# Softmax sums added up by DMA, and edge bits transposed off the matrix engine: one change to a four-layer graph kernel

## The chip, the core and the metric

The kernel runs on one core of a Trainium2 chip. A core has five engines that run their own instruction streams: TensorE (PE, matmuls; its weight loads are listed as PEld), VectorE (DVE), ScalarE (ACT), GpSimd (POOL) and SyncE (SP, which here only issues DMAs). PE writes into eight PSUM banks; the others work in SBUF and PSUM. The metric is the device time of one execution in microseconds: 2737.14 us, the median of three runs (2736.57 to 2737.26).

## The reference

64 graphs of 256 nodes with 256 features pass through four layers, each followed by `x = layernorm(x + layer(x, adj))`. Layer 0 is a transformer block with 8 heads of 32; the changed lines lie in its attention:

```python
allowed = (adj > 0) | (jnp.swapaxes(adj, 1, 2) > 0) | eye
qkv = x @ Wqkv.T + bqkv
scores = jnp.einsum('bhqd,bhkd->bhqk', q * scale, k)
scores = jnp.where(allowed[:, None], scores, -jnp.inf)
attn = jax.nn.softmax(scores, axis=-1)
ctx = jnp.einsum('bhqk,bhkd->bhqd', attn, v)
x = _layernorm(x + ctx @ Wo.T + bo, ln1_g, ln1_b)
ff = jax.nn.relu(x @ W1.T + b1) @ W2.T + b2
x = _layernorm(x + ff, ln2_g, ln2_b)
```

Layers 1 and 2 are single-head graph attention (a softmax over `leaky_relu(f_i + g_j)` where there is an edge), layer 3 is two relational graph convolutions. All products are f32. The mask `allowed` needs the edge matrix and its transpose.

## The kernel before

One graph is two row tiles of 128 nodes. `graph(g)` (line 757) writes down the operations of one graph: load, masks, attention, `wo`, layer norm, feed forward, two graph attention layers (`gat`), two convolutions (`conv`), the last layer norm and the store. Each operation goes into a `Plan` (line 128) with its engine, an assumed cost, the tiles it reads and writes and, for DMAs, a size and a lag. When all 64 graphs are written down, `Plan.schedule` orders them: it takes on each engine the operation with the smallest due time (`DUE`, one number for each kind of operation, plus `LATER`, one for each graph), no more than `WINDOW` ahead of the oldest, as soon as its buffers in the rings (`RINGS`, `SMALL`, `DRAM`) are free. PE's modes (`full`, `row`, `col`, `bits`, ...) carry assumed costs of switching. The instructions then stand in that order in each engine's queue, and every queue is executed in order. Seven to eight graphs are in flight at once, so that at any time PE works on matmuls of several layers of different graphs.

What the change touches:

- `masks` (901): `bits = adj > 0` in bf16 (DVE, L906); PE transposes its four 128x128 blocks into a bank `pt` (L911); `gm` (L914, for the graph attention layers) and `am = max(pt, bits)` (L915), then the diagonal (L920).
- `attention` (953): the scores are computed transposed (keys on partitions), eight heads in two groups `kt` of key tiles (L969, four row tiles of 32x128 side by side). ACT takes the exponential (L975), DVE multiplies by the mask (L977). `both[r]` is the sum over the two key tiles (L982, four DVE adds). `values` (987) is one PE operation: for each half `hg` of the heads four matmuls by a matrix of ones, 128 rows by 32 columns, which add `both` over the 128 partitions and put the sum on 32 partitions for each head (L991), then eight matmuls with `v` (L996). DVE takes the reciprocal of all 128x256 sums of each half (L1002) and multiplies (L1003). An ACT pass over `inv` (L1005) collects a number that is checked at the end of the program.
- `feed_forward` (1017): `x1` is turned for the next product, then multiplied by `ln1g` (L1022 by way of `with_row`, L782) and `b2` is added by DVE (L782 again).
- Helpers that the text speaks of: `add_later` and `add_row_later` (785, 789) add by a DMA with `accum_op=add`, issued by POOL (L787). `bounced` (818) transposes a tile without PE: DVE turns 32x32 blocks (L824), a DMA writes them to DRAM (`rows`, L827) and another reads them back in the right order (`T`, L832). `product` (870) issues all dense matmuls, so they all stand under L873. `layer_norm` (875) has four small POOL instructions (L887 to L890).

Of the kernel before, what the change touches and what calls it, by code (L numbers as in the profile page):

```python
# [11 lines left out]
BF16 = mybir.dt.bfloat16  # L12
# [14 lines left out]
FIRST_TURNED = 2  # L27
# [6 lines left out]
RINGS = {"x": 3, "adj": 4, "bits": 2, "am": 2, "gm": 6, "T": 4, "qk": 2, "v": 2, "p": 12, "both": 4, "inv": 1, "ctxT": 2, "X": 8,  # L34
         "xr": 1, "hid": 1, "h": 3, "e": 3, "n": 1, "rel": 3, "hi": 2, "lo": 2, "o": 4, "blocks": 1, "turned": 1, "xT": 2, "cols": 2, "pf": 3}
DRAM = {"rows": 8, "row": 6}
SMALL = {"mv": 8, "st": 4, "rstd": 8, "r": 6, "rdeg": 4}


WORTH, HOLD, WAIT, LOCK = 20.0, 0.0, 1000000.0, -0.5  # L40
WINDOW, FIRST, TAIL = 4.0, 6, 58
LANES = 8
DUE = [
    115.11, 130.1, 87.27, 113.55, 184.78, 267.91, 127.15, 3.7, 6.4, 850.28, 907.96, 17.01, 767.99, 288.87, 535.33, 276.68, 323.52, 314.8, 295.86, 329.82,
    300.15, 372.49, 286.87, 287.98, -502.68, 591.19, 64, 190.54, 194.31, 213.9, 713.3, 602.04, 241.89, 284.25, 282.43, 286.42, 332.5, 286.53, 340.1, 391.1,
    -896.08, 82.57, 223.73, 1512.3, 652.66, -43.08, 40.01, 326.22, 390.1, 385.75, 460.35, 501.93, 1085.72, 819.32, 729.09, 1434.36, 1462.97, 1572.86, 309.27, 377.7,
    422.98, 298.61, 489.54, 349.1, 349.77, 403.91, 409.77, 1039.63, 1164.93, 1206.11, 1047.88, 1793.82, 1345.99, 941.63, 462.04, -143.68, -426.28, -563.2, -305.02, 262.4,
    -8.54, -682.53, -1425.23, -878.48, -910.48, 17.76, -1230.15, -1241.9, -450.83, -995.94, -1138.75, -609.23, -940.48, -121.13, -36.53, 517.96, -269.05, 397.54, 54.48, 413,
    377.06, 153.19, 158.68, -378.26, 790.96, -31.03, 404.99, 300.98, 1238.57, 734.43, 1000.75, 626.51, 101.96, 382.13, 45.13, 270.56, -211.2, 112.91, -26.02, 715.95,
    909.95, 879.4, 1800.2, 738.61, -248.98, -17.6, 171.18, 86.17, 653.43, -436.69, 887.7, -60.25, 1415.03, -622.37, 760.39, 726.88, -39.87, 361.21, 51.78, -354.13,  # L50
    -811.15, -996.74, -21.07, -458.08, -355, -638.8, -301.25, -345.83, 35.99, -729.94, 342.61, 978.89, 501.93, 624.52, -156.62, 34.99, -355.8, -535.26, -1056.55, -853.61,
    -309.82, -604.29, -123.96, -430.91, 250.59, -935.54, -71.5, 785.28, 299.06, 741.23, 514.78, 1612.86, 44.41, -201.89, -507.28, 48.76, -1134.8, -1513.38, -738.99, -2121.1,
    -1887.25, -2427.69, -1547.71, -1074.55, -1743.55, -801.23, -1039.08, -1445.41, -1451.37, -1811.92, -1599.65, -1352.15, -803.41, 105.4, 51.2, -2.45, 905.11, 340.42, 479.09, 446.27,
    -346.11, -241.48, -1320.8, -1184.67, 227.95, -410.93, 181.58, 411.97, 33.28, 533.62, 973.02, 416.68, 625.02, -116.64, 219.42, -238.55, -103.18, 369.86, -1126.9, -254.14,
    -62.97, -478.61, -760.52, 195.37, 133.89, -1164.69, -221.19, 309.39, -223.51, -1384.43, -912.86, -586.25, -502.37, -752.61, -194.22, -177.7, -903.8, -82.98, 212.44, 450.15,
    -20.63, 600.03, 718.67, -372.99, -463.15, -655.56, -114.2, -441.38, -98.81, -1186.92, 2.55, 33.89, -212.9, 343.42, -941.93, -141.06, 434.71, -230.33, -762.23, -500.28,
    -737.15, -1236.95, 350.32, -429.54, 392.55, 735.93, -165.46, 17.17, -406.76, -280.33, -545.61, -118.67, -562.59, -662.05, -637.17, -123.17, -299.09, -894.99, -728.14, 308.8,
    -407.46, -591.06, -1279.97, -1171.47, -1185.92, -532.14, -839.14, -1199.67, -1382.19, -1710.49, -1500.13, -823.47, -1317.15, -1651.44, -1534.52, -1542.11, -1999.83, -2099.36, -2677.74, -1674.04,
    -2031.11, -886.93, -741.03, 141.07, -201.09, -665.49, -899.61, -1034.61, -519.13, 753.8, -330.91, 224.95, -439.11, -74.6, -388.8, 150.07, 320.46, 266.34, 661.45, -131.11,
    -575.29, -614.71, -909.95, -860.38, -218.26, -502.7, 299.21, -466.82, -157.72, -96.09, 95.71, -751.12, -80.72, -711.21, -1440.05, -1626.75, -1496.54, -701.82, -2131.37, -1553.57,  # L60
    -767.95, -883.9, -451.78, -721.17, -77.66, -81.75, -876.87, -264.16, -284.81, 164.33, 500.84, 572.97, 751.67, 221.66, -573.04, -421.79, -309.92, 661.24, -78.37, 822.6,
    402.49, 814.87, 925.8, 120.82, 1121.82, 521.23, 871.11, 987.71, 661.55, 675.71, 250.34, -481.05, -752.44, -688.49, -790.45, -353.78, -477.33, -799.05, -598.48, -834.15,
    135.16, 359.04, -419.04, -153.16, -427.9, -63.74, 206.11, 144.64, -396.59, 87.54, -508.49, 33.99, 247.18, -231.56, 116.24, 559.54, 113.68, 945.19, 114.83, 632.95,
    846.63, 23.88, 241.92, -60.66, 167.66, 426.06, -250.81, -25.85, -886.96, 163.03, 213.44, 144.25, -197.06, 214.87, 469.41, 48.09, 314.49, 729.23, 840.48, 272.15,
    949.87, -274.06, 407.94, 518.88, 627.68, -253.81, -324.22, 788.98, 182.1, 73.25, -283.59, -278.9, -438.37, -351.07, -11.1, 234.91, 791.22, 267.52, -262.82, 221.58,
    -55.85, -273.21, -716.88, -232.74, -243.65, -337.37, -686.64, 243.63, -363.44, 102.34, -294.19, 157.49, -122.58, 818.8, 167.06, -139.62, 564.19, 183.5, 40.04, 561.24,
    -469.96, -301.06, 183.9, -432.22, 344.47, -19.44, 175.22, -329.23, 111.52, 31.67, 0, 12.49, 16.35, 40.7, 13.03, 29.97, 79.66, 87.72, 88.16, 92.57,
    16.9, 42.2, 63.91, 67.37, 69.2, 69.57, 64.77, 66.51, 67.73, 68.1, 54.65, 63.05, 66.15, 90.74, 93.34, 103.29, 93.94, 113.24, 100.44, 111.1,
    101.32, 106.37, 89.66, 91.55, 102.68, 90.95, 92.88, 92.14, 95.53, 92.74, 96.15, 112.62, 115.22, 115.84, 108.16, 120.58, 126.02, 128.08, 123.52, 127.74,
    128.55, 132.38, 133.45, 134.52, 135.25, 136.34, 139.84, 156.74, 162.92, 141.05, 141.83, 146.74, 158.73, 159.93, 153.03, 155.22, 160.92, 162.78, 158.68, 159.54,  # L70
    161.3, 162.04, 154.36, 156.09, 161.67, 162.41, 156.95, 157.81, 160.55, 163.15, 165.1, 168.73, 172.37, 173.1, 174.18, 178.53, 179.69, 180.41, 181.13, 184.82,
    188.33, 190.19, 190.97, 195.88, 202.19, 203.65, 203.07, 206.36, 222.82, 225.76, 209.06, 211.91, 217.09, 223.82, 225.27, 228.89, 231.63, 234.38, 242.79, 245.03,
    235.73, 243.83, 244.01, 246.19, 248.14, 251.65, 257.58, 258.36, 263.28, 272.62, 274.23, 269.16, 273.95, 276.54, 341.81, 276.37, 276.67, 281.05, 288.88, 287.58,
    292.81, 294.47, 301.47, 303.32, 303.53, 307.8, 309.41, 309.85, 304.06, 309.25, 311.17, 313.08, 313.83, 318.66, 320.01, 324.08, 327.59, 217.6, 300.09, 321.45,
    331.08, 331.85, 336.77, 350.16, 352.09, 353.9, 355.27, 348.44, 350.37, 351.98, 353.57, 356.31, 359.28, 360.19, 360.79, 357.08, 357.99, 359.21, 361.32, 361.85,
    365.25, 366.27, 367.05, 374.16, 388.51, 395.12, 397.74, 400.66, 385.92, 388.51, 398.17, 401.4, 402.41, 406.64, 404.62, 407.66, 408.19, 415.16, 418.79, 420.65,
    446.91, 460.58, 469.56, 476.66, -42.08, -71.22, 47.55, 3.95, 87.01, -47.02, 84.87, 96.85, 43.29, 49.34, 127.81, 93.06, 163.1, 82.32, 60.43, 233.39,
    93.62, 90.44, -0.5, 120.06, -23.99, 59.25, 35.15, -243.24, 80.37, 53.47, 200.92, -73.58, -7.08, 5.9, -5.15, 25.23, 43.87, 9.22, -39.39, -39.72,
    -111.42, -25.63, 15.17, 9.26, 110.12, -23.73, 207.1, 32.19, 46.32, 175.57, 73.87, -13.49, 97.45, -54.1, 63.07, 26.32, 36.13, -21.71, 254.66, 142.72,
    97.69, 92.02, 135.98, 306.53, 204.66, 18, 8.92, 47.55, 119.05, -168.79, 195.29, 2.68, 311.48, 151.91, 107.66, 214.4, 509.65, 39.08, 110.14, 228.99,  # L80
    218.6, 168.24, 162.95, 261, 207.45, 107.57, 85.27, 116.9, 164.82, 190.13, 200.94, 178.43, 163.52, 204.35, 300.87, 365.21, 103.17, 173.45, 85.86, 207.98,
# [267 lines left out]
def tile_gnn_stack(ctx: ExitStack, tc: tile.TileContext, t: dict, out: bass.AP):  # L349
# [267 lines left out]
    def main_path(plan):  # L617
# [139 lines left out]
        def graph(g):  # L757
# [117 lines left out]
            def layer_norm(y):  # L875
# [21 lines left out]
                dve(0.88, stats, [y], [mv, stat])  # L897
                op("POOL", 1.8, root, [mv], [rstd], port="waits", lag=0.15)
                act(1.0, apply, [y, rstd], [y])

            def masks(adj):


# [570 lines left out]
```

## Time and profile before

| | |
|---|---|
| median of three runs | 2737.14 us |
| the profiled execution | 2740.2 us, of which its span 2738.3 us |
| PE / DVE / ACT / POOL busy | 99% / 90% / 58% / 34% of the span |
| sums by ones, L991 | 1024 records, 379 to 404 ns each |
| transposes of bits, L911 | 256 records, 219 ns |
| reciprocal, L1002 | 128 x 1729 ns |
| row adds and products, L782 | 192 x 671 to 672 ns |
| adding DMAs on POOL, L787 | 190, mean issue 942 to 1618 ns, landing 3.8 to 4.6 us after issue |
| DMA packets | 609611, mean 120 GB/s |

How to read it: the profile is one execution. Records of PE overlap, because matmuls are pipelined, so the distance from one start to the next says more than a record's length. An f32 matmul leaves two records, a bf16 one a single one. A list of waits gives, for an engine's instruction and the one that released it, the total in us, how many times, and the longest. A line of the timeline has start, duration, engine, line, operation, what it writes and reads, shape and count.

### The profile page before, as it was taken

Reading aid. Unit: us, or ns where it says so; the run is one execution under the profiler, and the core shown is the slowest. Engines: PE = TensorE matmul, PEld = TensorE weight load, DVE = VectorE, ACT = ScalarE, POOL = GpSimd, SP = SyncE. Lnnn points to the kernel's source line nnn. Section 1 sums busy time; section 2 is a strip of 40 time slices with the busy share of each in tenths; the row PEclk is TensorE's granted clock in tenths of the full one; section 3 lists DMA queues with packets and bytes.
Section 4 is the critical chain, followed back from the end, with each engine's and each line's share of the span. In section 5 each row is a group of like instructions: output and inputs, shape, how many; then the busy total and the mean of one; then the engine's idle time right before and its main releaser. Section 6 shows DMA issues by size and latency. Waiting matters only on the chain.

```text
span 2738.3 us, 48644 instructions
## 1 busy us (share of the span) xinstructions
PE 2712.7 (99%) x15808; PEld 2115.7 (77%) x15808; DVE 2465.2 (90%) x6538; ACT 1598.4 (58%) x3830; POOL 935.5 (34%) x1747
## 2 busy tenths in 40 slices
PE   8999999999999999999999999999999999999997
PEld 6887877777787787777777877877877777778774
DVE  6789989999999999999999999999999999988977
ACT  4446555556556556556555565565565555655767
POOL 2233333334333333333333333343333333332222
PEclk8999999999999999999999999999999999999999
DMA  7345545454454454554544544544545546364211
GB/s 187 95 110 130 130 116 129 119 127 123 127 135 120 128 130 121 129 124 129 133 120 124 139 119 125 135 121 127 129 121 132 125 128 147 97 143 108 51 47 40
DMA packets 609611, 329.91 MB, mean 120 GB/s; under 512 B 391694, under 2 KB 600616, under 8 KB 609352
## 3 DMA queue, kind: packets, MB, share of 16 engines
q1 hardware_dynamic: 564984, 275.72, 36.1%
q0 software_dynamic: 44368, 51.01, 11.9%
q8 instruction: 128, 2.10, 0.3%
q14 instruction: 131, 1.07, 0.1%
HBM read 182.60 MB, written 94.23 MB: 101 GB/s over the span
## 4 chain that ended last, share of the span: by engine, by line
PE 97%; DVE 1%; DMA 1%; ACT 1%; issue 0%; SPq 0%; POOL 0%; POOLq 0%
PE bank L873 80%; PE bank L969 5%; PE bank L1155 4%; PE bank L996 4%; PE bank L991 2%; PE bank L911 1%; DMA wqkv<-in_WqkvT_dram 0%; PE bank L802 0%; DMA rows<-turned 0%; ACT turned L813 0%; DVE p L977 0%; ACT e L1170 0%; DMA T<-rows 0%; DVE inv L1002 0%; ACT X L894 0%
## 5 line engine op out<-in xcount | busy, mean ns | idle before, releaser
L887 POOL TENSOR_SCALAR rstd<-mv 128x2 f32<-128x2 f32 x384 | 148.7, 387 | 1415.1 <-DVE mv L884 469.0
L873 PE MATMUL bank<-cw,T 128*128 128x512 f32 x1024 | 469.0, 592 | 0.0
L873 PE MATMUL bank<-T,w 128*128 128x256 f32 x2048 | 466.6, 380 | 0.0
L873 PE MATMUL bank<-w,hid 128*128 128x256 f32 x2048 | 457.0, 381 | 0.0
L873 PEld LDWEIGHTS bank<-w,hid 128*128 128x128 f32 x2048 | 397.0, 196 | 43.0 <-issue 3.4
L873 PEld LDWEIGHTS bank<-T,w 128*128 128x128 f32 x2048 | 384.8, 190 | 53.8 <-issue 2.0
L975 ACT ACTIVATE p<-bank 128x512 f32<-128x512 f32 x512 | 298.8, 603 | 169.9 <-PE bank L969 169.7
L894 ACT ACTIVATE X<-X,rstd 128x256 f32<-128x256 f32 x640 | 350.0, 599 | 78.1 <-POOL rstd L890 77.3
L977 DVE TENSOR_TENSOR p<-p,am 128x512 f32<-128x512 f32 x512 | 336.6, 681 | 27.4 <-ACT p L975 22.8
L888 POOL TENSOR_TENSOR rstd<-rstd,neghalf 128x2 f32<-128x2 f32 x384 | 315.0, 820 | 32.0
L873 PEld LDWEIGHTS bank<-cw,T 128*128 128x128 f32 x1024 | 198.8, 195 | 164.5 <-issue 144.8
L1031 ACT ACTIVATE hid<-bank,col_b 128x256 f32<-128x256 f32 x512 | 212.5, 469 | 105.3 <-PE bank L873 104.1
L873 PE MATMUL bank<-h,e 128*128 128x259 f32 x1024 | 264.3, 382 | 0.0
L873 PE MATMUL bank<-gw,T 128*128 128x258 f32 x1024 | 255.1, 381 | 0.0
L873 PE MATMUL bank<-xT,wqkv 128*128 128x256 f32 x1024 | 253.7, 385 | 0.9 <-DVE xT L865 0.9
L1002 DVE RECIPROCAL inv<-bank 128x256 f32<-128x256 f32 x128 | 217.2, 1729 | 30.7 <-PE bank L996 30.5
L882 DVE BATCH_NORM_STATS2 st<-X 128x6 f32<-128x256 f32 x640 | 238.3, 414 | 2.2
L873 PEld LDWEIGHTS bank<-gw,T 128*128 128x128 f32 x1024 | 198.8, 196 | 46.3 <-issue 24.6
L873 PEld LDWEIGHTS bank<-h,e 128*128 128x128 f32 x1024 | 186.5, 190 | 46.4 <-issue 14.9
L873 PEld LDWEIGHTS bank<-xT,wqkv 128*128 128x128 f32 x1024 | 193.0, 192 | 30.6 <-issue 2.5
L1155 PE MATMUL bank<-hi,rel 128*128 128x258 f32 (+1 forms) x512 | 182.6, 364 | 0.1
L824 DVE STREAM_TRANSPOSE turned<-X 128x512 f32<-128x512 f32 x236 | 166.1, 704 | 4.6 <-ACT X L894 3.1
(147 smaller groups left out, 4676.9 us busy)
## 6 DMA issues: line engine op xcount, KB each, us to landing
rows<-turned SPq DMA_DIRECT2D x295, 256.0 KB
T<-rows SPq DMA_DIRECT2D x295, 256.0 KB
adj<-in_adj_dram SPq DMA_DIRECT2D x128, 256.0 KB
x<-in_x_dram SPq DMA_DIRECT2D x64, 256.0 KB
xr<-in_x_dram SPq DMA_DIRECT2D x64, 256.0 KB
x<-row_bo POOLq DMA_DIRECT2D x64, 256.0 KB, 4.5
xr<-row_ln_b POOLq DMA_DIRECT2D x64, 256.0 KB, 3.8
out_dram<-o SPq DMA_DIRECT2D x64, 256.0 KB
```

The lines of the kernel that those rows point to most:

```text
L824: dve(0.63, lambda: nc.vector.transpose(turned().rearrange("p k (b n i) -> p (k b) i n", b=4, i=NB), xt().rearrange("p i (j c) -> p j i c" ...
L873: nc.tensor.matmul(dst, lhsT=lhs(c), rhs=rhs(c), start=(c == 0), stop=(c == n - 1))
L882: nc.vector.bn_stats(stat()[:, i, :], y()[:, i, :])
L887: nc.gpsimd.tensor_scalar(rstd()[:, 0, :], mv()[:, :, 1], 1.0, EPS, op0=ALU.mult, op1=ALU.add)
L888: nc.gpsimd.tensor_tensor(rstd()[:, 0, :], rstd()[:, 0, :], neghalf[:, 0:NB], op=ALU.pow)
L894: nc.scalar.activation(y()[:, i, :], y()[:, i, :], AF.Identity, bias=rstd()[:, 1, i : i + 1], scale=rstd()[:, 0, i : i + 1])
L969: nc.tensor.matmul(s[r]()[:, hg, :], lhsT=qk()[f, KB + hg, kt * P : (kt + 1) * P], rhs=qk()[f, hg, :], start=True, stop=True)
L975: act(0.58, lambda pr=pr, k=k, sr=s[r]: nc.scalar.activation(pr(), sr(), AF.Exp, accum_out=seen_sum[:, k : k + 1]), [s[r]], [pr])
L977: dve(0.60, lambda pr=pr, kt=kt: nc.vector.tensor_tensor(pr(), pr(), am()[:, kt, None, :].to_broadcast([P, KB, N]), op=ALU.mult), [pr, am] ...
L1002: dve(1.67, lambda hg=hg, pc=pc: nc.vector.reciprocal(inv()[:, hg, :], pc()[:, 1, :]), [pc], [(inv, hg)])
L1031: act(0.36, lambda f=f, k=k, ph=ph: nc.scalar.activation(hid()[:, f + k, :], ph()[:, k, :], AF.Relu, bias=b1[:, f + k : f + k + 1]), [ph, ...
L1155: nc.tensor.matmul(pa()[:, 0:n], lhsT=rel()[:, i, j * P : (j + 1) * P], rhs=part()[:, i, 0:n], start=(c == 0), stop=(c == len(terms) - 1))
```

## The change

1. **Sums.** `both` is now one tile that holds the four adds side by side. Two adding DMAs on POOL ("folds") add, for the first half of the heads, partitions 64 to 127 onto 0 to 63, and for the second half the other way. The sums matmuls then have 64 rows instead of 128 (the first half on rows 0 to 63, the second on 64 to 127), and all eight stand ahead of the values.
2. **Reciprocal.** The sums are the same on 32 partitions, so DVE transposes them in 32x32 blocks (two instructions), takes the reciprocal of one column of each block (128x16) and spreads the result with one more block transpose. ACT's pass reads the 128x16 tile.
3. **Bits.** From graph 4 on, PE no longer transposes `bits`. `bits_bounced` turns 32x32 blocks on DVE (two instructions), writes them to DRAM (`rows_b`) and reads them back (`pt`, in runs of 32 bf16 numbers, 64 bytes). `gm` and `am` then read `pt` from SBUF.
4. **b2** is added by a DMA (`add_row_later`) in place of a DVE add.
5. **Rings and order.** `both` 4 to 1 (of four times the size), `p` 12 to 11, `adj` 4 to 3, `pf` 3 to 2, `inv` gives way to `sums` (2) and `compact` (3), `turned_b` and `pt` 1 each, `rows_b` 4. `WORTH`, `HOLD`, `WINDOW`, all of `DUE` and `LATER` have new numbers, so the order of instructions on every engine is a new one.

```diff
-FIRST_TURNED = 2
+FIRST_TURNED, FIRST_BOUNCED = 2, 4
...
-WORTH, HOLD, WAIT, LOCK = 20.0, 0.0, 1000000.0, -0.5
-WINDOW, FIRST, TAIL = 4.0, 6, 58
+WORTH, HOLD, WAIT, LOCK = 38.41, 0.28, 1000000.0, -0.5
+WINDOW, FIRST, TAIL = 20.8, 6, 58
...
+            def bits_bounced(bits):
+                turned, rows, pt = new("turned_b", [P, NB, NB, P], BF16), new("rows_b", [4, P, P], BF16), tok("pt", BF16)
+                for k in range(NB):
+                    dve(0.35, lambda k=k: nc.vector.transpose(
+                        turned()[:, k].rearrange("p h (j c) -> p j h c", j=4),
+                        bits()[:, :, k * P : (k + 1) * P].rearrange("p h (a j) -> p j h a", j=4)), [bits], [(turned, k)], "uses")
+                op("SP", 0.5, lambda: nc.sync.dma_start(rows().rearrange("m p x -> p m x"),
+                                                        turned().rearrange("p k h x -> p (k h) x")), [turned], [rows],
+                   lag=SENT, size=0.5)
+                def back():
+                    r = rows()
+                    nc.sync.dma_start(pt().rearrange("p k (m c) -> p (k m) c", c=32),
+                                      bass.AP(tensor=r.tensor, offset=r.offset, ap=[[32, P], [32 * P, 16], [1, 32]]))
+                op("SP", 0.5, back, [rows], [pt], lag=BACK, size=1.1)
+                return pt
...
+                if g < FIRST_BOUNCED:
...
+                else:
+                    pt = bits_bounced(bits)
...
-                both = [new("both", [P, KB, N]) for r in range(4)]
+                both, half = new("both", [P, KB, 4, N]), P // 2
...
+                for hg in range(KB):
+                    into, out_of = slice(half * hg, half * hg + half), slice(half - half * hg, P - half * hg)
+                    op("POOL", 1.3, lambda hg=hg, into=into, out_of=out_of: nc.gpsimd.dma_start(
+                        both()[into, hg], both()[out_of, hg], accum_op=ALU.add),
+                       [(both, r) for r in range(4)], [(both, "lo" if hg else "hi")], lag=2.4, size=0.9)
...
                 def values():
                     for hg in range(KB):
+                        rows = slice(half * hg, half * hg + half)
+                        for r in range(4):
+                            nc.tensor.matmul(pcs[hg]()[32 * r : 32 * r + 32, 1, :], lhsT=ones[rows, :], rhs=both()[rows, hg, r, :],
+                                             start=True, stop=True)
+                    for hg in range(KB):
                         pc = pcs[hg]()
-                        for r in range(4):
-                            nc.tensor.matmul(pc[32 * r : 32 * r + 32, 1, :], lhsT=ones, rhs=both[r]()[:, hg, :],
-                                             start=True, stop=True)
...
-                pe("col", 2.58, values, [v] + both + list(p.values()), pcs, [ctxT, inv])
+                pe("col", 2.15, values, [v, both] + list(p.values()), pcs, [ctxT, compact])
                 for hg in range(KB):
                     pc = pcs[hg]
-                    dve(1.67, lambda hg=hg, pc=pc: nc.vector.reciprocal(inv()[:, hg, :], pc()[:, 1, :]), [pc], [(inv, hg)])
+                    dve(0.40, lambda hg=hg, pc=pc: nc.vector.transpose(sums()[:, hg, :], pc()[:, 1, :]), [pc], [(sums, hg)])
+                dve(0.17, lambda: nc.vector.reciprocal(compact(), sums().rearrange("p k (j d) -> p (k j) d", d=32)[:, :, 0]),
+                    [sums], [compact])
+                dve(0.63, lambda: nc.vector.transpose(inv().rearrange("p k n -> p (k n)"),
+                                                      compact()[:, :, None].to_broadcast([P, KB * N // 32, 32])),
+                    [compact], [inv], "uses")
...
-                act(0.62, lambda: nc.scalar.activation(inv(), inv(), AF.Identity, accum_out=seen_inv[:, g : g + 1]), [inv], [inv])
+                act(0.3, lambda: nc.scalar.activation(compact(), compact(), AF.Identity, accum_out=seen_inv[:, g : g + 1]),
+                    [compact], [compact])
...
-                with_row(x1, b2, ALU.add, [c_b2])
+                add_row_later(x1, b2, [c_b2])
```

## The prediction

> **What bounds the kernel now.** I read the shares of the engines first, then a table by stretches, then the list of what TensorE (PE) waited for, and last the timeline of one attention step.
>
> ```profile
> PE 2712.7 (99%) x15808; PEld 2115.7 (77%) x15808; DVE 2465.2 (90%) x6538; ACT 1598.4 (58%) x3830; POOL 935.5 (34%) x1747
> ```
>
> ```profile
> 400.00:2200.00 1800.00, 1800.00 (x10541) 1409.14 (x10540) 1660.14 (x4392) 1052.92 (x2550) 652.39 (x1166) 1.00 0.51 127
> ```
>
> ```profile
> PE bank L873 <- DMA wqkv<-in_WqkvT_dram: 3.8, 2, 2.3
> PE bank L873 <- DVE xT L865: 3.4, 2, 2.5
> PE bank L911 <- DVE bits L906: 2.0, 1, 2.0
> PE bank L802 <- ACT turned L813: 1.6, 4, 0.8
> ```
>
> The second fence gives stretch, length and the busy time of PE, PEld, DVE, ACT and POOL, then PE's clock, DMA share and GB/s. From 400 to 2200 us PE is busy for all 1800 us, at a granted clock of 1.00; asked for the same stretch, the list of PE's waits is empty. "Busy" alone proves little for pipelined matmuls, but the starts do: from one dense 128x256 record to the next is 0.216 us, without gaps, and the scores of successive graphs start 41.74 us apart. So in the middle a graph costs what PE's records take to issue, and the waits that the third fence begins (13.8 us in all, at the start and end) are the rest. What leaves PE's stream comes off the time, as long as nothing new makes PE wait. DVE is next: 1660.14/1800 x 41.74 = 38.5 us per graph.
>
> ```profile
> 1017.38 0.64 PE L991 MATMUL bank<-both,ones 128*32 128x256 f32 x8
> 1017.83 1.05 PE L996 MATMUL bank<-p,v 128*32 128x256 f32 x16
> 1018.70 0.61 PE L991 MATMUL bank<-both,ones 128*32 128x256 f32 x8
> 1019.13 1.05 PE L996 MATMUL bank<-p,v 128*32 128x256 f32 x16
> 1020.11 0.40 PE L911 MATMUL bank<-ident_b,bits 128*128 128x128 bf16 x4
> 1020.34 0.87 PE L873 MATMUL bank<-w,hid 128*128 128x256 f32 x3
> ```
>
> An f32 matmul is two records. The x8 of L991 are four matmuls side by side in four column tiles: the next line starts 0.45 us later (1017.38 to 1017.83), and 0.43 us later in the second group (1018.70 to 1019.13). So a group of four costs one slot of 0.432 us, and a graph has six slots here: two of sums, four of values.
>
> **The sums (64 graphs).** Two sums slots become one: eight matmuls of 64 rows x 32 columns, the two halves on different rows and different banks. That removes 0.432 us. The row tiling of the scores shows four tiles of 32 rows side by side (L969, starts 7 ns apart), the sums show four of 32 columns; no row has both at once. What is new is a change of tile shape inside the step, from 64x32 to 128x32. It has no row. Its lower end is 0. Its upper end is entering the row tiling: the start-to-start step grows from 0.216 to 0.309 us, and the next from 0.196 to 0.300: 0.197 us. The nearest row is entering the column tiling, where the same two steps are 0.309 and 0.220: 0.093 + 0.024 = 0.117 us, which I take. A gain beyond 0 has no reason. So 0.432 - 0.117 = 0.315 us a graph, 64 x 0.315 = 20.2 us (bounds 0.235 and 0.432: 15.0 and 27.6). [...]
>
> **The bits (60 graphs).** Four bf16 transposes leave PE. From the last column-tiled start to the second dense start is now 0.311 + 0.067 + 3 x 0.056 + 0.277 = 0.823 us. In eleven places where dense work follows the values directly it is 0.309 + 0.329 = 0.638. So 0.185 us a graph, 60 x 0.185 = 11.1 us; the four starts alone (0.235) would give 14.
>
> **What is added beside PE, per graph.** DVE loses two reciprocals of 1.729 (L1002) and one row add of 0.671 (L782, b2): -4.13. It gains four 128x256 transposes, priced between the 128x64 row (0.226) and the 128x512 row (0.704): 0.43 each, 1.72; a broadcast transpose, 0.704; a reciprocal of 16 columns, between 0.153 (1 column) and 1.729 (256): 0.25. Sum +2.67, net -1.46: 37.0 us against a period of 41.2, so DVE stays hidden. If each 128x256 transpose took the full 0.704 it would be 38.1, still hidden. gm and am read SBUF in place of a bank, at 0.414 and 0.390 at most as now. ACT loses 0.4 us.
>
> POOL gains three adding DMAs (two folds, b2), each 0.94 to 1.62 us by the L787 rows: about 3.9, from 15.1 to 19 us. SP gains two DMAs of 0.36 us each; in the new order they stand among the row and T bounces, and a T read queued behind them waits for 'rows_b' to land. DMA: by mean packet times of the trace, 512 packets of 256 B at 17.9 ns, 2048 of 64 B at about 11 (4 B take 9.0, 128 B 12.1), 256 adding ones of 1 KB at 106.5 and 128 of 4 KB at 2 x 203: 9 + 22 + 27 + 52 = 110 us over 16 engines, 6.9 us. The share goes from 51% to about 68%. [...]
>
> **The new wait.** The values on PE now wait for the second fold, not for the last DVE add. In the middle of the trace the first sums matmul starts 5.3 us after the last 'both' add ends. The built program's instruction order shows DVE with 35 instructions between that add and the first transpose of the sums: six statistics (0.414), six aggregates (0.173), four 512-wide ones near 0.67, two 512-wide transposes near 0.70, ten 256-wide ones near 0.45, three more near 0.41 and four small ones near 0.15: 14.0 us by their rows. Less 2.6 us for sums and values themselves, the fold has about 11.3 us. It needs a first issue of 1.3 us and a landing of 4.9 (o<-X, median; longest 6.3): 6.2 us, longest 7.6. So some 4 to 5 us of cover. Behind the folds on POOL stand a layer norm's four instructions and the b2 add; behind the waiting sums on PE stands everything. The bits have nearly a graph's time to come back: gm stands some 100 DVE instructions after the second transpose of its bits.
>
> From x1's product to the first w1 matmul the new order holds 17.0 us of PE work, priced by the rows, against 19.1; from a graph's first matmul to its last, some 327 both times. That 2.1 us is the thinnest cover that shrinks.
>
> **Sum.** 20.2 + 11.1 = 31.3 us. The profiled execution took 2740.2 us (span 2738.3), so it would take 2708.9. The median of the runs shown is 3.1 us lower (2737.1), and gives 2705.8. I leave the start and the end of the program at 0: there chains of ACT and DVE set the pace, with 2 us either way.
>
> **Rivals.** (1) The 64-row halves do not run side by side. For: no row shows eight tiles at once. Against: rows and columns each run four tiles at once. Then the eight take 0.864 and the change of shape stays: +7.5 us, less 11.1: 2733.5. This is the case that the change does not do what it says. (2) The fuller DMA rings make the bounced T tiles late, as in the 2.1 us above, and PE waits a little. For: 51% to 68%, and PE's queue is in order. Against: now SP waits 317 us in all for 'rows' to land (L832), and PE not once for a T read that came of it. A wait of 0.3 us in 60 graphs: +18, 2723.8. (3) Slower: the folds are late. Ahead of them on POOL stands the adding DMA to xr, which waits for its load; the list of waits has it at 27.3 us in 6 waits, longest 9.0. If the folds land more than 11.3 us after the last add, PE stands still for the excess in each graph: it decides from 5.1 us of delay, eats the whole gain at 5.6, and at 6.1 (1 us of excess in 58 graphs) gives 2764. Against: six such waits in 64 graphs.
>
> **Chances.** Forecast, PE still packed, 2698 to 2714: 0.60. Late bounces, about 2724: 0.14. No overlap of the halves, about 2734: 0.12. Late folds, over 2743: 0.14. About 0.2% (5.5 us) is what a measurement here can tell from no change: under 2731.6 faster 0.74, up to 2742.6 same 0.12, slower 0.14. The range goes from 2696 (shape change free, 2705.8 - 7.4, and 2 us at the end) to 2736 (takes in the second and third case), and leaves out 0.14.
>
> **What the next profile shows.** Right: PE busy 1800 of 1800 in the middle, the graphs 41.2 us apart, sums of a graph in x16 records within 0.45 us, the first value record 0.3 us after the second pass of the sums. Wrong about the halves: two groups of sums 0.43 us apart. Wrong about covers: waits of PE with T<-rows (bounces) or both<-both (folds) as releasers, in every graph. DVE above 39 us per graph, or POOL above 24, would show a mispriced term.

## The result and the profile after

The changed kernel takes 2750.94 us (median of 6 runs, 2745.96 to 2752.70) where the kernel before takes 2737.18 (6 runs, 2736.57 to 2737.46): ratio 1.0047, 95% interval 1.0036 to 1.0058. It is slower by 13.8 us; the forecast was 2706. The profiled execution took 2751.08 us, span 2749.3.

First the shares of the engines, then the stretches asked for in the prediction with the start and the end of the program beside the middle (columns as there):

```profile
PE 2697.2 (98%) x15568; PEld 2078.2 (76%) x15568; DVE 2369.8 (86%) x6722; ACT 1552.7 (56%) x3830; POOL 1062.6 (39%) x1939
```

```profile
0.00:100.00 100.00, 76.71 (x520) 57.98 (x521) 54.10 (x137) 34.69 (x98) 26.41 (x43) 0.86 0.75 167
400.00:2200.00 1800.00, 1793.98 (x10430) 1393.16 (x10432) 1604.84 (x4542) 1020.41 (x2555) 717.57 (x1305) 1.00 0.69 153
2400.00:2749.30 349.30, 330.33 (x1755) 242.49 (x1746) 277.17 (x833) 220.62 (x481) 118.90 (x243) 0.98 0.39 87
```

The kernel before, asked for its first 100 us:

```profile
0.00:100.00 100.00, 88.86 (x610) 69.73 (x614) 67.84 (x145) 46.53 (x131) 24.69 (x41) 0.91 0.59 151
```

PE's total fell by only 15.5 us, and its idle time doubled, from 25.6 to 52.1 us of the span. In the first 100 us PE is busy for 76.7 us instead of 88.9, with a lower clock (0.86 against 0.91), and the DMA engines are busier (0.75 against 0.59). The middle is nearly packed, with 6 us missing. So the loss lies mostly outside the stretch that the prediction was worked out from.

The list of PE's waits over the whole program begins:

```profile
PE bank L1031 <- DMA both<-both: 11.8, 7, 4.8
PE bank L944 <- DVE bits L937: 8.4, 1, 8.4
PE bank L682 <- DMA T<-in_b_dram: 4.3, 1, 4.3
PE bank L1031 <- DVE X L1160: 2.1, 1, 2.1
PE bank L884 <- DMA T<-rows: 1.8, 5, 0.8
```

The waits for the folds (L1031) are few, seven in 64 graphs. Three of them, 7.3 us, lie before 100 us. The step itself does what was forecast. In the middle of the trace of after:

```profile
987.29 0.66 PE L1031 MATMUL bank<-both,ones 64*32 64x256 f32 x16
987.88 1.93 PE L1038 MATMUL bank<-p,v 128*32 128x256 f32 x32
```

All 16 records of the sums start within 0.28 us (eight starts 6 to 7 ns apart, 0.194 us, eight more), so eight 64x32 tiles run side by side. The values follow 0.59 us after the first start.

The table places the time. The ratios are against executions of the kernel before made beside each run, whose medians lie between 2736.99 and 2737.98. "g14" is the start of graph 14's sums in the timeline, "14-56" the time from there to graph 56's, "tail" the rest of the span. "Step" is the usual distance from one graph's sums to the next one's. The parts come from one profiled execution each. Executions of the changed kernel differ by 6.7 us among themselves, so a part is good to a few us only.

| kernel | median us (runs) | ratio to before, 95% | g14 | 14-56 | tail | step |
|---|---|---|---|---|---|---|
| before | 2737.18 (6) | | 558.3 | 1751.0 | 428.9 | 41.73 |
| after | 2750.94 (6) | 1.0036 to 1.0058 | 571.6 | 1742.9 | 434.9 | 41.28 |
| rows_moved | 2746.25 (7) | 1.0023 to 1.0046 | 573.1 | 1738.0 | 432.1 | 41.28 |
| no_fold | 2740.87 (10) | 1.0005 to 1.0024 | 557.7 | 1750.2 | 429.3 | 41.55 |
| no_bounce | 2736.69 (10) | 0.9986 to 1.0005 | 568.9 | 1735.2 | 431.6 | 41.28 |
| rows_nofold8 | 2735.92 (10) | 0.9986 to 1.0005 | 561.0 | 1739.2 | 438.0 | 41.28 |
| nofold14 | 2731.38 (10) | 0.9970 to 0.9989 | 559.8 | 1737.3 | 431.8 | 41.29 |
| flat_back | 2741.90 (10) | 1.0011 to 1.0030 | 569.6 | 1735.3 | 431.9 | 41.29 |
| pt_on_act | 2744.90 (9) | 1.0016 to 1.0037 | 573.2 | 1736.7 | 433.4 | 41.29 |
| bare_order | 2739.50 (10) | 0.9997 to 1.0016 | 561.8 | 1746.1 | 429.1 | 41.55 |
| nofold14_pt | 2731.34 (11) | 0.9970 to 0.9988 | 558.7 | 1735.9 | 429.5 | 41.29 |
| ends_pt | 2729.28 (7) | 0.9960 to 0.9982 | 562.1 | 1737.7 | 429.4 | 41.29 |
| ends_pt_sp | 2732.58 (11) | 0.9974 to 0.9992 | 563.3 | 1736.9 | 429.8 | 41.29 |
| before_rows_early | 2740.68 (11) | 1.0004 to 1.0022 | 558.4 | 1751.0 | 429.0 | 41.73 |
| fold_unwaited | 2748.13 (5) | 1.0029 to 1.0057 | 566.9 | 1748.6 | 430.9 | 41.55 |
| ends_pt_rows | 2729.62 (6) | 0.9957 to 0.9981 | 560.8 | 1737.7 | 429.2 | 41.29 |
| ends6_pt_rows | 2732.43 (11) | 0.9967 to 0.9985 | 561.9 | 1737.9 | 431.9 | 41.29 |

Had the step's gain of 0.45 us a graph come off everywhere, after would show 552, 1732 and 425. So this execution lost about 20 us before graph 14, 11 between 14 and 56, and 10 in the tail.

### The profile page after: what moved, and what is told of

The parts are those of the page before. It is cut to its first block, busy times and chain, and to the rows that moved or that the text cites. A ratio compares the mean times of both kernels' runs of the same rounds, so it can differ in the third digit from the quotient of the medians.

```text
span 2749.3 us, 48921 instructions
## 1 busy us (share of the span) xinstructions
PE 2697.2 (98%) x15568; PEld 2078.2 (76%) x15568; DVE 2369.8 (86%) x6722; ACT 1552.7 (56%) x3830; POOL 1062.6 (39%) x1939
## 4 chain that ended last, share of the span: by engine, by line
PE 86%; DVE 5%; DMA 4%; issue 2%; ACT 1%; POOL 1%; SPq 0%; POOLq 0%; DVEq 0%; ACTq 0%
PE bank L884 72%; PE bank L1038 4%; PE bank L1004 4%; PE bank L1205 4%; DMA both<-both 2%; PE bank L1031 1%; DMA T<-rows 1%; DVE p L1012 1%; DVE both L1017 1%; DMA rows<-turned 1%; DVE st L893 0%; DMA o<-X 0%; PE bank L813 0%; DVE turned L835 0%; DVE X L1064 0%
## 5 line engine op out<-in xcount | busy, mean ns | idle before, releaser
L898 POOL TENSOR_SCALAR rstd<-mv 128x2 f32<-128x2 f32 x384 | 112.1, 292 | 976.7 <-DVE mv L895 874.5
L1012 DVE TENSOR_TENSOR p<-p,am 128x512 f32<-128x512 f32 x512 | 331.0, 680 | 14.4 <-ACT p L1010 11.9
L899 POOL TENSOR_TENSOR rstd<-rstd,neghalf 128x2 f32<-128x2 f32 x384 | 302.2, 787 | 32.0
L1021 POOL DMA_DIRECT2D both<-both x128 | 110.0, 999 | 384.6 <-DVE rdeg L1211 148.8
L1081 ACT ACTIVATE hid<-bank,col_b 128x256 f32<-128x256 f32 x512 | 218.1, 472 | 68.9 <-PE bank L884 68.1
L884 PE MATMUL bank<-h,e 128*128 128x259 f32 x1024 | 255.6, 383 | 0.3 <-ACT e L1136 0.3
L884 PEld LDWEIGHTS bank<-h,e 128*128 128x128 f32 x1024 | 192.2, 190 | 44.8 <-issue 10.5
L1192 ACT CAST hi<-bank 128x256 fp32r<-128x256 f32 x256 | 94.8, 372 | 172.8 <-PE bank L884 172.3
```

Of the source, the lines that this page charges most:

```text
L884: nc.tensor.matmul(dst, lhsT=lhs(c), rhs=rhs(c), start=(c == 0), stop=(c == n - 1))
L898: nc.gpsimd.tensor_scalar(rstd()[:, 0, :], mv()[:, :, 1], 1.0, EPS, op0=ALU.mult, op1=ALU.add)
L899: nc.gpsimd.tensor_tensor(rstd()[:, 0, :], rstd()[:, 0, :], neghalf[:, 0:NB], op=ALU.pow)
L1012: dve(0.60, lambda pr=pr, kt=kt: nc.vector.tensor_tensor(pr(), pr(), am()[:, kt, None, :].to_broadcast([P, KB, N]), op=ALU.mult), [pr, am] ...
L1021: op("POOL", 1.3, lambda hg=hg, into=into, out_of=out_of: nc.gpsimd.dma_start(both()[into, hg], both()[out_of, hg], accum_op=ALU.add), [(b ...
L1081: act(0.36, lambda f=f, k=k, ph=ph: nc.scalar.activation(hid()[:, f + k, :], ph()[:, k, :], AF.Relu, bias=b1[:, f + k : f + k + 1]), [ph, ...
```

## The experiments

All of them except before_rows_early are edits of the changed kernel that keep its plan and the order of each engine's queue, apart from what is named. The first theory was that the early row loads lose the start, since the trace showed the first adjacency late behind them. The rivals were the folds and the bounces.

### rows_moved: the row loads put back

```diff
-        for o in plan.schedule():
-            o.issue()
+        for o in rest[:place] + late[:3] + rest[place:sums] + late[3:] + rest[sums:]:
+            o.issue()          # late: loads of ln1_b, b2, cb2 (at 24 us), sum of b2 (at 45 us)
```

> The changed kernel with one thing put back: the three row loads (ln1_b, b2, cb2) that its order issues on POOL at 5.6 to 6.7 us are issued at about 25 us, as before, and the small DVE sum of b2 after them; nothing else is moved. Theory 1, the lost time is lost at the start: the early row loads hold the DMA engines from 6 to 16 us, the first adjacency lands 14 us late (bits at 18.2 us instead of 4.2), PE's first dense work comes at 19.1 us instead of 8.8. Then the waits bank<-DVE bits (8.4 us) and bank<-T<-in_b (4.3 us) go, the dense work starts near 9 us, and the time falls by some 8 to 12 us, to about 2741. Theory 2, the loss is the folds' and the bounces': the start catches up later, because the first graphs wait for their own chains anyway, and the time stays at 2749 to 2752.

2746.25 us, 4.7 under the changed kernel, with overlapping intervals. The wait for bits fell from 8.4 to 1.6 us, but a wait for wqkv of 3.8 us came in its place, and graph 14 was no earlier (573.1). The first theory fell as the main cause: another load was now the late one. The 8.4 us are in part that one execution's: in no_fold and nofold14, whose instructions are the same up to there, the wait for bits is 3.1 us.

### no_fold: the folds out

```diff
-    nc.gpsimd.dma_start(both()[into, hg], both()[out_of, hg], accum_op=ALU.add)
+    None
-    lhsT=ones[rows, :], rhs=both()[rows, hg, r, :]
+    lhsT=ones, rhs=both()[:, hg, r, :]
```

> The changed kernel, same order on every engine, but the two folds issue nothing and the sums take all 128 rows again, as two groups. Nothing else differs. PE gets its slot back: the values step rises from 2.35 to 2.62 us, 64 x 0.267 = 17.1 us. If PE is packed and the folds are covered: 2751 + 17 = 2768, less the 11.8 us that PE waits for folds in four places: 2756. If the folds and their transfers are what makes the kernel slow (contention, late T reads), the time falls under 2751 in spite of the longer step, to 2745 or less.

2740.87 us: 10 us faster, although every graph takes 0.27 us longer (step 41.55). Graph 14 comes 13.9 us earlier. The folds cost more than they bring: 10.1 + 64 x 0.27 = 27 us, against the 17 us of the shorter step.

### no_bounce: the bounces of the bits out

```diff
-    pt = bits_bounced(bits)            # two DVE transposes, write, read-back
+    # same operations in the plan, nothing issued; gm and am read a constant of ones in place of pt
```

> The changed kernel, same order, but from graph 4 on the two block transposes of the bits and their two transfers issue nothing; both masks read a constant of ones instead, so the masks of these graphs are left out. DVE loses 0.9 us and the DMA engines some 31 us of packets per graph. Theory 1 (the start is the cause): the time stays within 2 us, 2749 to 2751, less the 1.8 us of waits for rows. Theory 2 (the bounces crowd the transfers, 64 B pieces above all): the middle's waits go, and the time falls by 6 us or more, to 2745 or less.

2736.69 us: 14 us faster. Graph 14 stays late (568.9); the gain is in 14-56, which has 1.4 us above a step of 41.28 in place of 9.1, and the tail. So folds and bounces seem to do their harm in different places. How much of the 9.1 is the bounces' own is not shown: rows_moved and nofold14 have the same instructions between graphs 14 and 56 as the changed kernel, bounces and folds included, and stand 4.2 and 3.5 us above the same sum.

### rows_nofold8: the row loads back, and folds only from graph 8 on

```diff
+    # as rows_moved, and:
-    both()[into, hg], both()[out_of, hg], accum_op=ALU.add)
+    both()[into, hg], both()[out_of, hg], accum_op=ALU.add) if g >= 8 else None
-    lhsT=ones[rows, :], rhs=both()[rows, hg, r, :]
+    lhsT=ones[rows, :] if g >= 8 else ones, rhs=both()[rows if g >= 8 else slice(0, P), hg, r, :]
```

> The three row loads put back to 25 us, and in graphs 0 to 7 the folds issue nothing and the sums take 128 rows; graphs 8 to 63 fold. The first folds wait some 8.5 us on PE in the changed kernel, because with few graphs in flight nothing covers a fold's 6 us. Eight graphs pay 0.267 us each, 2.1 us. Theory 1: 6 us under the run with the row loads alone, about 2735. Rival: these waits hide others (the chains of the first graphs, DVE and ACT), so only the 2 us are paid and the time is that of the other run or 2 us more.

2735.92 us, 10.3 under rows_moved: theory 1. Graph 14 comes at 561.0 instead of 573.1.

The timeline shows what the first two folds do to PE. After, around graphs 0 and 1:

```profile
43.37 2.29 PE L759 MATMUL bank<-spread_ln_b,w 128*128 128x1 f32 x20
47.22 1.20 PE L1031 MATMUL bank<-both,ones 64*32 64x256 f32 x16 [1.56 <-DMA both<-both]
48.36 3.64 PE L1038 MATMUL bank<-p,v 128*32 128x256 f32 x32
...
67.80 1.08 PE L1031 MATMUL bank<-both,ones 64*32 64x256 f32 x8 [4.79 <-DMA both<-both]
69.86 1.08 PE L1031 MATMUL bank<-both,ones 64*32 64x256 f32 x8 [0.99 <-DMA both<-both]
70.87 3.10 PE L1038 MATMUL bank<-p,v 128*32 128x256 f32 x32
```

The same step of graph 0 without folds (no_fold):

```profile
44.06 1.07 PE L1030 MATMUL bank<-both,ones 128*32 128x256 f32 x16
44.95 1.91 PE L1037 MATMUL bank<-p,v 128*32 128x256 f32 x32
```

The brackets hold the idle time and its releaser. A wait of 1.6 to 6 us is not all: the 32 values records behind it take 3.64 and 3.10 us instead of 1.91. The stretches around the first wait (columns: PE busy, clock, DMA share, GB/s) say why:

```profile
44.00:46.00 2.00, 1.66 (x15) 1.00 1.22 219
46.00:53.00 7.00, 5.78 (x60) 0.51 1.05 285
53.00:56.00 3.00, 3.00 (x32) 1.00 0.64 160
```

The clock granted to PE was halved (0.50) from 46.0 to 52.8 us. It fell during the wait, and not after it: PE stood still for only 1.56 us, behind 2.3 us of one-column matmuls (L759). The wait by itself does not decide it. In two other runs the same place looks as follows, first in bare_order (no folds, so no wait), then in flat_back (folds as in the changed kernel):

```profile
44.05 1.94 PE L1022 MATMUL bank<-both,ones 128*32 128x256 f32 x16
45.75 2.74 PE L1029 MATMUL bank<-p,v 128*32 128x256 f32 x32
```

```profile
45.71 0.76 PE L1031 MATMUL bank<-both,ones 64*32 64x256 f32 x16 [1.32 <-DMA both<-both]
46.40 1.93 PE L1038 MATMUL bank<-p,v 128*32 128x256 f32 x32
```

Without a wait the sums of bare_order took 1.94 us and the values 2.74, where no_fold's took 1.07 and 1.91; from the first start of the sums to that of the values it is 1.70 us instead of 0.89, about half the pace. With a wait of 1.32 us the sums of flat_back took 0.76 us and the values 1.93, close to the 0.66 and 1.93 of the changed kernel's middle. So the wait neither suffices nor is needed; what else decides it is not shown. At the second fold of the changed kernel, with 4.8 and 1.0 us of waiting, the clock was 0.50 from 67.8 to 73.0 us.

The folds themselves, on DVE and POOL of after:

```profile
34.30 2.49 DVE L1017 TENSOR_TENSOR both<-p 128x512 f32<-128x512 f32 x4
37.10 0.92 POOL L1021 DMA_DIRECT2D both<-both  x1 [29.87 <-DVE both L1017]
37.67 2.85 POOL L798 DMA_DIRECT2D x<-row_bo  x2
39.16 2.28 POOL L1021 DMA_DIRECT2D both<-both  x1
```

The adds end at 36.8 us and the sums can start at 47.2: 10.4 us for a fold that the prediction put at 6.2, with the second issue taking 2.28 us. Between the two issues stand two other adding DMAs of POOL (`x<-row_bo`), and from 40 to 48 us the DMA share (packet times added up, over the time of 16 engines) is 1.15: the first graphs' and weights' loads are under way. How much of the 10.4 us each of these makes up is not shown. In the middle the same rows are:

```profile
1019.26 0.67 DVE L1017 TENSOR_TENSOR both<-p 128x512 f32<-128x512 f32 x1
1020.49 1.69 POOL L1021 DMA_DIRECT2D both<-both  x2 [6.60 <-DVE rdeg L1211]
1029.30 0.66 PE L1031 MATMUL bank<-both,ones 64*32 64x256 f32 x16
```

From the end of the adds PE's sums follow after 9.4 us here (9.2 in the median of graphs 14 to 55), and the second fold has landed after 7.0 in the median: some 2 us to spare, where the prediction counted on 4 to 5.

### nofold14: folds only from graph 14 on, row loads left early

```diff
+    # as the fold lines of rows_nofold8, with g >= 14
```

> The changed kernel, same order, row loads as they are; graphs 0 to 13 do not fold (their two folds issue nothing, their sums take 128 rows), graphs 14 to 63 fold. In the changed kernel the values step of graph 14 comes at 571.6 us, in the kernel before at 558.3, with no fold at all at 557.7. Theory A, the folds lose the start: with no cover yet in the first graphs PE waits for them, its clock falls, and what follows is late: graph 14 comes near 558, and the time falls by some 13 us, to about 2738. Theory B, the row loads lose the start: with them still early, graph 14 stays above 565 and the time above 2744.

2731.38 us, ratio 0.9979 (0.9970 to 0.9989): 19.6 us under the changed kernel and faster than the kernel before. Theory A, by more than expected. Of the 19.6, 11.8 lie before graph 14; the rest is in the middle and the tail, where this kernel has the same instructions as the changed one. That part is not explained; it is not far above the spread of single executions.

### flat_back: the read-back in one piece of 1 KB per partition

```diff
-    nc.sync.dma_start(pt().rearrange("p k (m c) -> p (k m) c", c=32),
-                      bass.AP(..., ap=[[32, P], [32 * P, 16], [1, 32]]))
+    nc.sync.dma_start(pt().rearrange("p k n -> p (k n)"), bass.AP(..., ap=[[512, P], [1, 512]]))
```

> The changed kernel, same order, but the bits are read back from DRAM as one piece of 1 KB for each partition in place of sixteen pieces of 64 B: the same bytes, a sixteenth of the pieces, the same waits. (The edges so read stand at wrong places, so the masks from graph 4 on are others.) Theory A, the 64 B pieces fill the queue, and the T reads behind them are issued late (20 of the 216 issues of T<-rows between 600 and 2400 us take over 1 us, where the kernel without bounces has 3 and the kernel before none): these long issues go, the values steps keep 41.28 us, and the time comes within 3 us of the kernel without bounces, 2737 to 2740. Theory B, what costs is the bounce's bytes, its write, or VectorE's two transposes: the time stays at 2746 to 2751.

2741.90 us, 9 us under the changed kernel, above the interval of 2737 to 2740 but nearer to it. 14-56 is as short as without any bounce (1735.3). Issues of T<-rows over 1 us fell from 20 to 2.

### pt_on_act: the read-back issued by ScalarE

```diff
-    nc.sync.dma_start(pt()...
+    nc.scalar.dma_start(pt()...
```

> The changed kernel with one word changed: the read-back of the bits in 64 B pieces is issued by ScalarE instead of SyncE, so it stands in another queue than the T reads. Theory A (a full queue): the T reads are no longer held up at their issue, and the time falls as without the pieces, to 2738 to 2743, unless ScalarE's wait for the bits' write costs something. Theory B (the 2048 pieces take the DMA engines' time, whichever queue they come from): no change, 2748 to 2751.

2744.90 us, 6 us under. 14-56 is 1736.7, and one issue of T<-rows is over 1 us. Theory A for the middle; the start (573.2) and so the time stay above the expected.

The rows behind these two, for the issue of T<-rows between 600 and 2400 us (minimum/median/maximum in ns): after, pt_on_act and the kernel before:

```profile
L843 SPq DMA_DIRECT2D T<-rows x216: 354/360/1853, 606.5 to 2397.6; - x108
```

```profile
L843 SPq DMA_DIRECT2D T<-rows x217: 354/360/1279, 608.1 to 2399.6; - x109
```

```profile
L832 SPq DMA_DIRECT2D T<-rows x216: 359/363/473, 602.1 to 2397.7; - x108
```

One such case of after, in order:

```profile
1009.77 0.49 SPq L927 DMA_DIRECT2D pt<-rows_b  x1
...
1012.03 1.84 SPq L843 DMA_DIRECT2D T<-rows  x1
...
1018.75 3.48 PE L884 MATMUL bank<-T,w 128*128 128x256 f32 x15 [0.52 <-DMA T<-rows]
```

The 2048 pieces of `pt` are issued in 0.49 us; the next read in the same queue then takes 1.84 us to issue, and PE waits for it at the first `w1` matmul, the place that the prediction called the thinnest cover. Of the 20 long issues, 17 stand directly behind a read of `pt`. But they do not cost the same everywhere: no_fold has 21 of them, and its bounces cost only 1.4 us (against bare_order, below); nofold14 has 22.

### bare_order: neither transfer, the rest of the change alone

```diff
+    # the edits of no_fold and no_bounce together
```

> The changed kernel's order on every engine without either edit's transfers: folds issue nothing and the sums take 128 rows, and from graph 4 on the bits are neither turned nor bounced (both masks read ones, so the masks of these graphs are left out). PE then has the bits' 0.18 us a graph less than before: 11 us. If the order itself costs nothing, 2737 - 11 = 2726. If the new order loses at the start by itself (the values of graph 0 come at 44 us in every run of it, at 34 before), some 6 us more: 2732. Without the bounces alone it was 2736.7, without the folds alone 2740.9; if the two losses add up, 2751 - 14 - 10 = 2727.

2739.50 us, not 2727 to 2732. PE has 0.175 us a graph less than before (41.73 to 41.555), 10.5 us in 60 graphs, so 2726.7 was due: what is left of the change costs 12.8. That is the new order, but also the new rings, the short reciprocal and the DMA for `b2`, which this run keeps; no run separates them, and "order" below stands for all of these. By the parts, with 0.175 us taken off for each bounced graph, 5 lie before graph 14, 2 in 14-56 and 2 in the tail; the remaining 3 to 4 cannot be placed, because the kernel before's profiled execution was itself 3.1 above its median. The two losses do not add up either: without folds the bounces cost 1.4 (2740.87 - 2739.50), with them 14.2.

### fold_unwaited: the folds' transfers, without the wait

```diff
-    nc.gpsimd.dma_start(both()[into, hg], both()[out_of, hg], accum_op=ALU.add)
+    nc.gpsimd.dma_start(aside[hg], both()[out_of, hg], accum_op=ALU.add)      # aside: DRAM, not read
-    lhsT=ones[rows, :], rhs=both()[rows, hg, r, :]
+    lhsT=ones, rhs=both()[:, hg, r, :]
```

> The changed kernel, same order; the two folds of every graph are still issued and move the same bytes out of the same rows, but they add into a spare piece of DRAM that nobody reads, and the sums take 128 rows. So the transfers stay and PE's wait for them goes; the slot comes back (0.267 us a graph). Without any fold the time was 2740.9 and graph 14's values came at 557.7. Theory A (the wait): graph 14 comes at 558 to 562, the time is 2741 to 2744. Theory B (the traffic): graph 14 stays near 571 + 3.7, and the time is 2755 or more, since the slot is lost too.

2748.13 us, between the two: both theories hold in part. The transfers cost 2748.1 - 2740.9 = 7 us. The wait costs 2750.9 + 17.3 - 2748.1 = 20 us, with 17.3 = 64 x 0.27 for the slot that this kernel pays. These are estimates: the five executions of this kernel lie 6 us apart, and PE's list of waits has only 11.8 us for folds. Into DRAM a fold's landing is a little longer (median 5.2 us against 4.9), so the 7 may be somewhat high.

### nofold14_pt, ends_pt, ends6_pt_rows: where a fold is covered

```diff
+    # nofold14_pt: the edits of nofold14 and pt_on_act
+    # ends_pt: the same with 14 <= g < 57 for the folds
+    # ends6_pt_rows: the same with 6 <= g < 57, and the edit of rows_moved
```

> The kernel without folds in graphs 0 to 13, and the 64 B read-back issued by ScalarE. With both the middle has no cause of stalls left that the runs so far show: values steps at 41.30 us between graphs 14 and 56 (41.36 without the read-back moved, 41.50 in the changed kernel). 42 x 0.06 = 2.6 us, and some in the tail: 2728. If the two remedies do not add up, because folds crowd the transfers themselves: 2731 as without the read-back moved.

2731.34 us: the read-back on ScalarE added nothing to nofold14 (2731.38). Without the early folds the long issues (22 over 1 us in nofold14, one here) hardly matter to the time.

> As the run before (no folds in graphs 0 to 13, read-back issued by ScalarE), and no folds from graph 57 on either. Seven graphs pay 0.267 us, 1.9 us. Theory 1, the folds lose time in the tail as in the start, for want of other graphs to cover them (between 2400 us and the end the changed kernel's PE stands still longest for a values step): 3 to 5 us come back, net 2 to 3 under the run before, about 2725. Theory 2, the tail's chains hide the folds: 2 us more than the run before, 2730.

2729.28 us, ratio 0.9971 (0.9960 to 0.9982), the fastest kernel of all. The 2 us are within the intervals of both: no verdict on the tail.

> As the run before, but the folds begin with graph 6 in place of 14: eight graphs more with the shorter step, 8 x 0.267 = 2.1 us. If a fold is covered as soon as the first graphs overlap (PE's waits for folds of the changed kernel before 100 us are 6 of its 11.8): 2 us less than the run before. If graphs 6 to 13 still expose part of it (3.6 us of waits for folds between 100 and 600 us): the same or 2 us more.

2732.43 us against 2729.62 with folds from 14 on: eight more folds bring nothing, as in the second case; the intervals overlap.

### ends_pt_sp, before_rows_early, ends_pt_rows: the first loads

```diff
+    # ends_pt_sp: SyncE's first 19 loads: x, adj, wqkv, adj, wqkv, x, xr, wo, w1, ..., gw, cw last
+    # before_rows_early: the kernel before, ln1_b, b2, cb2 loaded right after bo
+    # ends_pt_rows: ends_pt with the edit of rows_moved
```

> As the run before, and SyncE's first 19 loads in an order like that of the kernel before: both adjacencies and graph 0's x ahead, the loads of cw and gw (issued from 8.3 to 17 us, 5.6 and 3.2 us long) behind w1 and wo. Theory 1, the new order of the first loads loses some 5 us at the start (without either edit's transfers graph 14's values come at 561.8 us, where 558.3 less the bits' 2 are due): the first values come some 4 to 9 us earlier than 44 us, and the time falls by 4 to 5, to about 2721. Theory 2, the first loads are bound by the transfers' sum, whatever their order: no change.

2732.58 us, 3 above ends_pt, and the first sums at 47.4 us instead of 44.2: PE now waits 7.2 us for wqkv. No gain, as theory 2 said; but the first values did not come earlier, as the test of theory 1 needed, so another order of these loads is not ruled out.

> The kernel before, with its three row loads (cb2, b2, ln1_b) issued on POOL right after the row bo, at about 6 us in place of 26 to 28, as the changed kernel does; nothing else. Theory 1 (the start is lost to these loads, by holding up the first adjacency and the first weights): PE's first dense work comes later than 8.8 us, and the time rises by 3 us or more, to 2740 or more. Theory 2 (as putting them back in the changed kernel left graph 14 where it was, they only shift which load is waited for): 2736 to 2738.

2740.68 us, 3.5 above the kernel before beside it (2737.23): theory 1's size. But graph 14 moves by only 0.1 us in the profiles, because the kernel before's profiled execution is one of its long ones.

> The fastest kernel so far (no folds in graphs 0 to 13 and from 57 on, read-back issued by ScalarE; 2729.3) with the three row loads moved back to 25 us. Theory 1 (the early row loads cost the start 3 to 5 us, as the times of the two runs that move them say): 2725 to 2726. Theory 2 (they only change which load is waited for): 2728 to 2731.

2729.62 against 2729.28: theory 2. So the row loads cost 3 us in the kernel before, perhaps 5 in the changed one and nothing in ends_pt; their effect depends on which load is late otherwise, and stays open.

## Why the prediction was wrong

- **The step that failed** is "I leave the start and the end of the program at 0 ... with 2 us either way". It forecast a time for the whole program from a stretch in which seven or eight graphs cover each other. The new order, with the rings, the reciprocal and `b2` that come with it, costs 12.8 us by itself (bare_order); of the 9 that the parts can place, 7 lie at the ends. Nor did chains of ACT and DVE set the pace at the start: of the changed kernel's waits of PE there, the longest end with folds (7.3 us), with a load (4.3) and with `bits`, whose adjacency landed late (8.4). I had its list of instructions, but priced no load and no chain of the first graphs. The folds and the bounces then cost another 28.7 us, partly in the middle, where the forecast had put new waits at nothing.
- **The fold's cover** (11.3 against 6.2 us) held in the middle, though by less than forecast (9.2 against 7.0): the waits for `both` there are 2.5 us in 1800. The row that it took the landing from, `o<-X`, has a median of 4.6 us and not 4.9. The cover was applied to all 64 graphs. At the start the folds took 10.4 and 6.9 us, the second no longer than in the middle, and too little covered them; a halved clock came on top (0.50 from 46.0 to 52.8 us). With the bounces present the folds cost 27 us (20 waiting, 7 in transfers) against a gain of 17.3. The third rival had late folds, but in every graph and behind the adding DMA to `xr`; PE waited for them in seven places, and at graph 0 two adding DMAs to `x` stood between the folds.
- **The bounces** were weighed by the time of their packets. The DMA share came out as forecast (0.69 against 68%), but at least part of the harm came from the queue: behind a read of 2048 pieces the next read was issued late (up to 1.85 us for the issue instead of 0.36), and moving that read to another queue gave 6 us, larger pieces 9. The pieces were of 64 B, and of 1 KB in flat_back; no run here reads `pt` in a size between them. The second rival (late bounces, priced 18 us) had the place right, but not the form: PE waits for T reads five times, 1.8 us in all, and not in every graph. In the changed kernel the bounces cost 14.2 us, without folds 1.4; the way from late reads to most of the 14.2 stays open.
- **The sums**: side by side, as forecast; rival 1 is out. The gain is 0.27 us a graph instead of 0.315: the change of tile shape costs 0.16 and not 0.117. From the start of the last sums record to that of the first values record it is 0.306 us, where it is 0.194 between the two rounds of sums. 17.3 us in place of 20.2.
- **The bits**: 0.175 us against 0.185, 10.5 us in place of 11.1. Right.
- **DVE, POOL**: 1604.84/1800 x 41.28 = 36.8 us a graph against 37.0 forecast; POOL 16.5 against 19. Right, and they nearly hide: 2.3 us of PE's waits between 400 and 2200 us end with DVE, none with POOL's own work.

The sum by medians: 2705.8 forecast; 3.5 that the two terms are smaller (31.3 against 27.8); 12.8 order; 14.5 folds without bounces (2736.7 - 2739.5 + 17.3); 14.2 bounces on top: 2750.8, measured 2750.9. The sum closes because its terms are differences of these same runs; it says where the time went and not how. What is open: which part of the order costs the 5 us before graph 14, since neither the row loads nor the one other order of SyncE's first loads gave them back; why folds and bounces cost more together; and why nofold14 gains in the middle too.

## What to carry to other kernels

A saving per item that is paid for with latency must be checked where there are few items in flight: count the cover of the first and the last graphs by their own rows, and give them the old form (here folds only from graph 14 on turned +13.8 us into -5.6, and with none from 57 on and the read-back on another queue into -8). A transfer of many small pieces is priced by what stands behind it in its queue too, and not by its share of the engines alone (here 2048 pieces of 64 B, and behind them an issue of up to 1.85 us instead of 0.36). Where an edit brings a new order, the order is an edit of its own and is worth a run without the others.

## What was not expected of the hardware

- PE's clock halved where PE hardly stood still: around a wait of 1.56 us it was 0.50 for 6.8 us, and 32 records took 3.64 us in place of 1.91; in bare_order these records took 2.74 us at the same place with no wait at all, behind 2.3 us of one-column matmuls, and in flat_back 1.93 with a wait of 1.32 us.
- A read of 128 KB in 64 B pieces was issued in 0.49 us, and the next one in the queue took up to 1.85 us instead of 0.36.
- Loads of one 1 KB row to 128 partitions, four at once at the start, had packets of 4 KB that took 845 ns in the median (159 to 2447), where the kernel before's four, between 31 and 37 us, took 159.
